# A four-layer graph network on one core: first pair transposed by TensorE, wk on SyncE's queue, half-array steps counted by the scheduler, leads by stage at the end

## The chip, the cores and the metric

The kernel runs on one core of one Trainium2 chip. A core has five engines, each with its own instruction stream: TensorE (PE, matrix multiplication, with weight loads shown apart as PEld), VectorE (DVE), ScalarE (ACT), GpSimd (POOL) and SyncE (SP), which here only issues DMAs. Streams are in order: an instruction that waits holds everything behind it on its engine. The metric is the device time of one execution in microseconds, lower is better; the time before is the median of three runs.

## The reference

`x` has 128 batches of a 128 x 512 matrix in fp32, `adj` is one 128 x 128 matrix shared by all batches and layers. Four layers follow each other, each with a residual and a layer norm.

```python
def reference(x, adj, b0, Wq, bq, Wk, bk, Wv, bv, Wo, bo, W, a, beta, weight, bias):
    # layer 0: out = max_j relu(A[:, None, :] + (C - A)[:, :, None]), A = adj @ x, C = A + b0
    x = layernorm(x + L0(x, adj, adj, b0))
    # layer 1: attention, 8 heads of 64
    q, k, v = (x @ Wq + bq), (x @ Wk + bk), (x @ Wv + bv)          # per head
    s = q @ k.T / sqrt(64) + (1 - adj) * -1e9
    x = layernorm(x + (softmax(s) @ v) @ Wo + bo)
    # layer 2: graph attention
    h = x @ W
    e = leaky_relu((h @ a[:512])[:, None] + (h @ a[512:])[None, :], 0.2) * adj
    x = layernorm(x + elu(softmax(e) @ h + beta * h))
    # layer 3: graph convolution, norm_adj = D^-1/2 adj D^-1/2
    x = layernorm(x + norm_adj @ (x @ weight) + bias)
    return x
```

Since in layer 0 the second operand is `adj` as well, the maximum over j is a row maximum of `adj @ x` plus a bias, and that is how the kernel computes it.

## The kernel before

Batches are worked in pairs (64 pairs, named by their even batch). Each batch passes through some hundred named steps; a step is one Python function that issues the instructions of one stage for one batch or pair. The steps on TensorE are:

- `A` (L733): `adj @ x`, two matmuls of 128 x 512.
- `QP1` to `QP7`, the same with `K`, `V`, `Y`, `U`, `Z` (all L644, in `seven`): a 256 x 512 by 512 x 512 product for a pair, done with seven half-size products in place of eight. `Y` is the product with Wo, `U` that with layer 2's W, `Z` that with layer 3's weight. Each step is 8 matmuls of 128 x 128 x 128 (`Q`, `K`) or 4 of 128 x 128 x 256 (the others). The seven products need differences of the weights, made once (`QT`, `KT`, ... four subtractions, L601 to L604), and sums of the operand (`XS1` to `XS4`, `YS1` ..., L620, on GpSimd). Results go into three small groups of PSUM tiles (`px` 1, `py` 2, `pz` 1), which ScalarE and VectorE read and combine (`u`, `U2`, `U3`, `C11` to `C22`, L657 to L703).
- `SC` (L807): the scores of one batch, 16 matmuls that contract over 64 rows only, two heads at a time in the two row halves of the array.
- `O` (L882): probabilities by v, 16 matmuls that fill 64 columns only, two heads in the two column halves.
- `E`, `BT` (L929, L967): one transpose each; `GT` (L980) and `NX` (L1027): 8 matmuls each, layer 2's attention by x and layer 3's norm_adj by x.

Between them lie the layer norms (`ST0`/`Y1`/`U3`/`Z1` on VectorE, `Q0` to `Q3` and `AP0` to `AP3` on ScalarE, `P0` to `P3` on GpSimd), the softmaxes (`M`, `SM1`, `EXP`, `SMR`, `SMN`), layer 2's logits (`L`, `EZ`, `E1`, `EE`, `E2`, `BE`), its elu (`U1`, `UE`, `U2`, `UP`) and evacuations (`OE`, `GE`, `NE`).

**Transposes by way of DRAM.** The layer-0 output of a batch is transposed thus: `MX1` (L757) stores it to DRAM in `dx`, `MX2` (L763) loads it back with four DMAs in 32-row blocks into `xB`, and `TX` (L782) transposes the blocks on VectorE into `xT`, which Q, K and V read. The probabilities go the same way (`MS1`, `MS2`, `TS`). `RL` (L771) loads a pair's `dx` a second time, as the residual `x2`, to which `C1` (L775, GpSimd) adds a bias row that `ROW` (TensorE, L493) and `ROW1` make from bv, Wo and bo.

**The order of the work** is written by a planner that runs while the program is built, `list_order`. Each `Step` has an engine, a cost in us, steps that it comes after (some with a delay in planned time), and buffers that it takes from `POOLS`. The planner places one step at a time: the one that can start earliest by its costs; on TensorE ties go by `rank` (`LAG`, a due time in batches for each step name), on the others by readiness less `soon`. The order that results is the instruction order of each engine; the delays and costs exist in the planner alone, and on the chip an instruction starts when its operands and buffers are there.

All x loads and transposes, and the weights from Wv on (`FETCH`), are issued by SyncE; Wq is issued by ScalarE at the start (L424), and the four DMAs of Wk by ScalarE after `AP0` of batch 1.

Of the kernel before, what the change touches and what calls it, by code (L numbers as in the profile page):

```python
# [23 lines left out]
SIGNAL = 0.2  # L24


class Step:
# [8 lines left out]
    def __init__(self, engine, cost, *after, takes=(), soon=0.0, batches=None, port=False):  # L36
        self.port = port or engine == "POOL"
        self.engine, self.cost, self.after = engine, cost, after
        self.takes, self.soon = dict(takes), soon
        self.batches = batches or (lambda b: True)  # L40
# [17 lines left out]
def list_order(steps, rank, pools, n):  # L58
# [13 lines left out]
    free, ends, taken, order = {}, {}, {p: [] for p in pools}, []  # L72
    while todo:
        best = None
        for k in can:
# [8 lines left out]
            key = (t, rank(*k) if s.engine == "PE" else ready[k] - s.soon, k)  # L84
# [5 lines left out]
        ends[k] = free[s.engine] = t + s.cost  # L90
# [24 lines left out]
def second(b):  # L115
    return b == 1
# [3 lines left out]
    "px": 1, "py": 2, "pz": 1, "tr": 2, "sc": 1, "x": 3, "xB": 2, "xT": 2,  # L120
    "qT": 2, "kT": 1, "v": 2, "s": 1,
    "sB": 1, "sT": 1, "oT": 1, "x2": 2, "z": 1, "e": 2, "bT": 2, "gT": 1, "m": 1, "x3": 2,
# [17 lines left out]
    "LD": Step("SP", 0.4, "LD-1", "MX1-2", takes={"x": ("MX1",)}),  # L140
# [7 lines left out]
    "AP0": Step("ACT", 1.03, "P0+"),  # L148
    "MX1": Step("SP", 0.4, "AP0", "MX1-1", takes={"dx": ("MX2+", "RL")}),
    "MX2": Step("SP", 1.8, ("MX1", 2.1), takes={"xB": ("TX",)}),  # L150
    "RL": Step("SP", 0.4, ("MX1+", 2.1), takes={"x2": ("UP+",)}, batches=even),
    "C1": Step("POOL", 1.27, ("RL+", 3.0), "ROW1@"),
    "TX": Step("DVE", 0.65, ("MX2", 2.9), "TX-1"),
    "SC": Step("PE", 1.2, takes={"sc": ("M",)}),
# [8 lines left out]
    "O": Step("PE", 1.15, "TS", "VE", "O-1", takes={"tr": ("OE",), "oT": ("Y+",)}),  # L163
# [33 lines left out]
    "WV0 WV1 WV2 WV3 WO0 WO1 WO2 WO3 BV BO W20 W21 W22 W23 A0 A1 BETA W30 W31 W32 W33 B3"  # L197
).split()
for i, name in enumerate(FETCH):
    STEPS[name] = Step("SP", 0.4, (FETCH[i - 1], 1.4) if i else "MX2+", batches=first)  # L200
STEPS["TX"].takes = {"xT": ()}

for i in range(4):
    STEPS[f"WK{i}"] = Step("ACT", 0.1, "AP0" if i == 0 else f"WK{i-1}", batches=second)
# [11 lines left out]
def seven_steps(n, sums, needs, weights, pool, out, add=(), turned=False, copy=False, T="POOL"):  # L216
# [20 lines left out]
    step("P1", "PE", c, "S1", *needs, (n + "T@",), takes={  # L237
        "px": (n + "C11",), "u": (last,), **({"uL": (n + "C21",)} if turned else {}), **out
    })
    step("P6", "PE", c, "S2", "P1", takes={"py": (n + "C21",)})  # L240
# [29 lines left out]
for n, needs, letters in (  # L270
    ("X", ["TX+"], "QKV"), ("Y", ["OE+"], "Y"), ("U", ["GE+"], "U"), ("Z", ["NE+"], "Z")
):
    sum_steps(n, needs, readers_of(*letters))
done = {
    "Q": seven_steps("Q", "X", ["TX+", "BQ@"], [("ADJ1", 9.0)], "xT", {"qT": ("SC+",)},
                     turned=True, T="DVE"),
    "K": seven_steps("K", "X", ["TX+", "BQ@"], [("WK3@", 4.0)], "xT", {"kT": ("SC+",)}, turned=True),
    "V": seven_steps("V", "X", ["TX+"], [("WV3", 4.0)], "xT", {"v": ("O+",)}, copy=True),
# [12 lines left out]
    "A": 0.484, "VP4": 4.350, "KP6": 4.536, "QP3": 6.105, "KP2": 6.393, "QP6": 6.543,  # L291
    "QP7": 6.580, "QP2": 6.783, "QP1": 6.839, "KP1": 7.155, "QP4": 7.239, "KP3": 7.490,
    "QP5": 7.598, "KP4": 7.761, "VP1": 7.807, "KP5": 7.914, "KP7": 8.090, "VP6": 8.158,
    "VP7": 8.220, "VP2": 8.342, "SC": 8.342, "VP5": 8.615, "VP3": 9.057, "O": 10.588,
    "YP5": 11.378, "YP7": 12.212, "YP1": 12.323, "YP6": 12.631, "YP2": 13.017,
    "YP4": 13.081, "YP3": 13.224, "E": 13.481, "UP5": 13.618, "BT": 13.636, "GT": 13.682,
    "UP6": 14.401, "UP2": 14.576, "UP4": 14.618, "UP3": 14.739, "UP1": 15.409,
    "UP7": 15.488, "NX": 16.433, "ZP4": 16.536, "ZP3": 16.847, "ZP6": 17.306, "ZP1": 17.589,
    "ZP2": 17.729, "ZP7": 18.238, "ZP5": 18.291,
}  # L300

LEAD = {}
# [9 lines left out]
def kernel(  # L312
# [464 lines left out]
    def TX(b):  # L777
        if b % 2 == 0:
            xT[b] = buf("xT", [P, C, 2 * P], b)
            xT[b + 1] = xT[b]  # L780
# [342 lines left out]
```

## Time and profile before

| what | value |
|---|---|
| median of three runs | 3124.65 us (3120.0, 3124.65, 3124.87) |
| the profiled execution, own time | 3119.54 us |
| its span in the trace | 3117.8 us |
| TensorE busy | 3062.5 us, 98% of the span |
| VectorE, ScalarE, GpSimd busy | 75%, 70%, 55% |
| mean granted TensorE clock | 0.996 |
| DMA | 313.45 MB, mean 101 GB/s |

The span runs from the first to the last instruction of the program, and the profiled execution's own time is 1.7 us more. Busy time of an engine counts its instructions alone. Matmuls overlap each other in the records (each is listed as longer than the distance to the next), so the distance from the start of one step to the start of the next is the better measure of what a step costs TensorE.

### The profile page before, as it was taken

How to read it: one execution, taken by the hardware profiler on the slowest of the kernel's cores; microseconds unless marked ns; L12 is line 12 of the kernel's file. 1: busy time of each engine (PE TensorE's matmuls, PEld its weight loads, DVE VectorE, ACT ScalarE, POOL GpSimd, SP SyncE). 2: the span in 40 equal slices, each digit the busy share in tenths (PEclk: the TensorE clock that was granted, in tenths of full speed). 3: DMA queues.
4: the chain of work that ended last, by engine and by line, in shares of the span. 5: the costliest groups of instructions: out<-in, count | busy, mean ns of one | idle time of the engine just before them, and what ended most of it. 6: DMA issues, size and time to landing. Idle time of an engine off the chain costs nothing.

```text
span 3117.8 us, 61619 instructions
## 1 busy us (share of the span) xinstructions
PE 3062.5 (98%) x21010; PEld 2704.0 (87%) x21010; DVE 2335.9 (75%) x5410; ACT 2196.1 (70%) x7234; POOL 1721.3 (55%) x1950
## 2 busy tenths in 40 slices
PE   7999999999999999999999999999999999999996
PEld 5888888888888888888888888888888888888975
DVE  5777777777777777777777777777777777777774
ACT  3677777776776777777777767767777777776664
POOL 4455555555555555555555555555556555555465
PEclk9999999999999999999999999999999999999998
DMA  7333332332323323333323223233233333232120
GB/s 209 124 109 100 105 100 91 109 102 95 107 94 106 102 95 104 100 100 104 102 90 111 99 96 107 94 105 102 96 104 100 102 103 102 91 111 85 62 73 29
DMA packets 236763, 313.45 MB, mean 101 GB/s; under 512 B 27936, under 2 KB 159136, under 8 KB 236448
## 3 DMA queue, kind: packets, MB, share of 16 engines
q1 hardware_dynamic: 234096, 307.40, 29.8%
q8 instruction: 166, 2.72, 0.4%
q10 hardware_dynamic: 2352, 2.10, 0.3%
q14 instruction: 149, 1.22, 0.1%
HBM read 175.18 MB, written 134.22 MB: 99 GB/s over the span
## 4 chain that ended last, share of the span: by engine, by line
PE 95%; DVE 2%; ACT 1%; POOL 1%; issue 1%; DMA 0%; SPq 0%; POOLq 0%; DVEq 0%; ACTq 0%
PE py_U L644 6%; PE py_Q L644 6%; PE py_K L644 5%; PE py_V L644 5%; PE py_Y L644 5%; PE py_Z L644 5%; PE ps_s L807 4%; PE ps_nx L1027 4%; PE ps_o L882 4%; PE px_Q L644 4%; PE px_U L644 4%; PE pz_Q L644 4%; PE pz_K L644 4%; PE pz_V L644 4%; PE ps_gT L980 4%; PE px_V L644 4%
## 5 line engine op out<-in xcount | busy, mean ns | idle before, releaser
L578 ACT ACTIVATE x<-x,off,rstd 128x512 f32<-128x512 f32 x512 | 416.6, 814 | 17.1
L838 ACT ACTIVATE s<-s,mx 128x128 f32<-128x128 f32 x1024 | 395.2, 388 | 7.2 <-issue 3.7
L550 DVE BATCH_NORM_STATS2 st<-x 128x6 f32<-128x512 f32 x512 | 346.5, 677 | 12.8 <-DMA x<-in_x 7.7
L573 POOL TENSOR_TENSOR rstd<-rstd,neg_half 128x2 f32<-128x2 f32 x256 | 178.8, 698 | 288.5 <-ACT rstd L559 288.0
L852 ACT ACTIVATE s<-s,sm 128x128 f32<-128x128 f32 x1024 | 313.0, 398 | 1.2 <-DVE sm L847 1.1
L1041 POOL TENSOR_TENSOR x<-x,b_bc 128x512 f32<-128x512 f32 x128 | 178.2, 1393 | 196.2 <-PE ps_nx L1027 196.2
L620 POOL TENSOR_TENSOR SX_V<-xT 128x256 f32<-128x256 f32 x128 | 93.3, 729 | 298.7 <-DVE sm L847 271.0
L916 DVE SCALAR_TENSOR_TENSOR junk<-x,wa_bc 128x512 bf16<-128x512 f32 x256 | 233.4, 912 | 32.3 <-ACT x L578 20.8
L1008 POOL TENSOR_TENSOR x<-x,x 128x512 f32<-128x512 f32 x128 | 162.9, 1272 | 76.2 <-DVE x L1004 67.8
L892 ACT COPY oT<-ps_o 128x512 f32<-128x512 f32 x128 | 75.0, 586 | 183.7 <-PE ps_o L882 182.1
L838 ACT ACTIVATION_READ_ACCUMULATOR s<-s,mx 128x1 f32 x1024 | 192.4, 188 | 0.0
L620 POOL TENSOR_TENSOR S_Y<-oT 128x256 f32<-128x256 f32 x128 | 93.8, 732 | 162.1 <-PE pz_U L644 157.4
L775 POOL TENSOR_TENSOR x<-x,bo_bc 128x512 f32<-128x512 f32 x128 | 160.4, 1275 | 24.5 <-DMA x<-dx 24.3
L577 ACT ACTIVATE off<-off,rstd 128x1 f32<-128x1 f32 x512 | 147.5, 288 | 27.4 <-POOL rstd L573 24.0
L823 DVE TENSOR_TENSOR s<-ps_s,mask 128x512 f32<-128x512 f32 x256 | 164.1, 681 | 1.8 <-PE ps_s L807 1.8
L703 DVE TENSOR_TENSOR x<-py_Y,x 128x256 f32<-128x256 f32 x192 | 81.5, 424 | 109.4 <-PE py_Y L644 82.9
L644 PEld LDWEIGHTS px_K<-xT,wk_sb 128*128 128x128 f32 x1024 | 133.7, 192 | 31.2 <-issue 27.0
L872 DVE STREAM_TRANSPOSE sT<-sB 128x1024 f32<-128x1024 f32 x128 | 158.1, 1235 | 0.8 <-PE ps_o L882 0.7
L1027 PE MATMUL ps_nx<-naT,x 128*128 128x128 f32 x1024 | 145.8, 288 | 13.0 <-ACT x L578 12.6
L807 PEld LDWEIGHTS ps_s<-kT,qT 64*128 64x128 f32 x2048 | 124.2, 187 | 38.4 <-issue 37.3
L832 DVE TENSOR_REDUCE mx<-s 128x8 f32<-128x1024 f32 x128 | 155.4, 1214 | 2.0
L1027 PEld LDWEIGHTS ps_nx<-naT,x 128*128 128x128 f32 x1024 | 133.7, 198 | 24.2 <-ACT x L578 13.6
(182 smaller groups left out, 9226.4 us busy)
## 6 DMA issues: line engine op xcount, KB each, us to landing
dp<-s SPq DMA_DIRECT2D x128, 512.0 KB, 2.6
sB<-dp SPq DMA_DIRECT2D x512, 128.0 KB, 2.8
x<-in_x SPq DMA_DIRECT2D x128, 256.0 KB, 3.3
dx<-x SPq DMA_DIRECT2D x128, 256.0 KB, 2.7
xB<-dx SPq DMA_DIRECT2D x512, 64.0 KB, 2.0
x<-dx SPq DMA_DIRECT2D x64, 512.0 KB, 3.2
out_x<-x SPq DMA_DIRECT2D x128, 256.0 KB, 2.0
wq_sb<-in_L_gnn_Wq ACTq DMA_DIRECT2D x4, 256.0 KB, 6.3
```

The costliest lines, as they stand in the source:

```text
L550: nc.vector.bn_stats(st, t)
L573: nc.gpsimd.tensor_tensor(r, r, neg_half.to_broadcast([P, 2]), ALU.pow)
L578: nc.scalar.activation(dst, src, AF.Identity, bias=shift, scale=scale)
L620: nc.gpsimd.tensor_tensor(s[:, i], x, y, op)
L644: nc.tensor.matmul(to, lhsT=one, rhs=two, start=(new and k == 0), stop=(k == 1), skip_group_check=True,)
L807: nc.tensor.matmul(scores[b][par][:, c, :], lhsT=qT[b][rows, c, cols], rhs=kT[b][rows, c, cols], start=True, stop=True,)
L823: nc.vector.tensor_tensor(by_head(s)[:, par * C : (par + 1) * C], ps.rearrange("p h (q s) -> p h q s", s=S), mask.rearrange("p (q s) -> p ...
L838: nc.scalar.activation(s[:, :, h], s[:, :, h], AF.Exp, bias=mx[:, h : h + 1], accum_out=sums[b][:, h : h + 1],)
L852: nc.scalar.activation(s[:, :, h], s[:, :, h], AF.Identity, scale=sm[:, h : h + 1])
L916: nc.vector.scalar_tensor_tensor(junk, x2[b][:, b % 2], 1.0, wa_bc[i], op0=ALU.mult, op1=ALU.mult, accum_out=s12[b][:, i : i + 1],)
L1027: nc.tensor.matmul(ps[:, c, :], lhsT=x3[b][:, b % 2, c * P : (c + 1) * P], rhs=naT, start=True, stop=True,)
L1041: nc.gpsimd.tensor_tensor(t, t, b3_bc, ALU.add)
```

## The change

There are four parts, and a new plan that comes from them.

1. **The first pair (batches 0 and 1) no longer goes through DRAM to be transposed.** `PX` (VectorE) copies x into the column order that `xT` has, `PT` (TensorE) makes four 128 x 128 transposes into one PSUM tile, and `PTE` (VectorE) copies that to `xT`. `MX2` and `TX` are left to batches from 2 on. `MX1` stays for all batches, since `RL` reads `dx`.
2. **The four DMAs of Wk move** from ScalarE's queue (after `AP0` of batch 1) to the head of `FETCH` on SyncE's queue; the planner starts `FETCH` after the first two x loads plus 4 us, each piece 1.3 us after the one before, and no longer after `MX2` of the first pair. `KT`, the weight differences of K, moves from GpSimd to VectorE.
3. **The planner knows half-array steps.** `SC` has the mode "row", `O` the mode "col", all others "". A step whose mode differs from the one before it on TensorE costs `SWITCH` = 0.1 us more in the plan (the costs of `SC` and `O` themselves are lowered from 1.2 and 1.15 to 1.09 and 1.02), and while a mode is on, another step with a mode is ranked `CLOSE` = 0.5 batches earlier.
4. **New due times.** `LAG` is replaced, and `LEAD`, empty before, holds values for single stages of pairs 56 to 63.

Beside these: four x buffers for three, three `x2` for two; `LD` waits in the plan for `LD` of two batches before plus 8 us in place of `MX1`; `MX2` is priced at 2.6 for 1.8; the need of the weight differences goes from `P1` to `P6`.

In the new order of instructions on TensorE, an `O` stands directly before an `SC` 104 times and an `SC` directly before an `O` 3 times; in the old one the latter happens twice and the former never. All other steps are the same in number, with 2 x 4 transposes added.

```diff
-    def __init__(self, engine, cost, *after, takes=(), soon=0.0, batches=None, port=False):
+    def __init__(self, engine, cost, *after, takes=(), soon=0.0, batches=None, port=False, mode=""):
...
-            key = (t, rank(*k) if s.engine == "PE" else ready[k] - s.soon, k)
+            if s.engine == "PE":
+                key = (t, rank(*k) - (CLOSE if mode and s.mode else 0.0), k)
+            else:
+                key = (t, ready[k] - s.soon, k)
...
-        ends[k] = free[s.engine] = t + s.cost
+        ends[k] = t + s.cost
+        if s.engine == "PE" and s.mode != mode:
+            ends[k] += SWITCH
+            mode = s.mode
+        free[s.engine] = ends[k]
...
-    "px": 1, "py": 2, "pz": 1, "tr": 2, "sc": 1, "x": 3, "xB": 2, "xT": 2,
+    "px": 1, "py": 2, "pz": 1, "tr": 2, "sc": 1, "x": 4, "xB": 2, "xT": 2,
...
-    "LD": Step("SP", 0.4, "LD-1", "MX1-2", takes={"x": ("MX1",)}),
+    "LD": Step("SP", 0.4, "LD-1", ("LD-2", 8.0), takes={"x": ("MX1", "PX")}),
...
-    "MX2": Step("SP", 1.8, ("MX1", 2.1), takes={"xB": ("TX",)}),
+
+    "PX": Step("DVE", 0.6, "AP0", takes={"xB": ("PT",)}, soon=20, batches=early, port=True),
+    "PT": Step("PE", 0.5, "PX", takes={"tr": ("PTE",)}, batches=early),
+    "PTE": Step("DVE", 0.65, "PT", "PTE-1", soon=20, batches=early),
+    "MX2": Step("SP", 2.6, ("MX1", 2.1), takes={"xB": ("TX",)}, batches=late),
...
-    "TX": Step("DVE", 0.65, ("MX2", 2.9), "TX-1"),
-    "SC": Step("PE", 1.2, takes={"sc": ("M",)}),
+    "TX": Step("DVE", 0.65, ("MX2", 2.9), "TX-1", batches=late),
+    "SC": Step("PE", 1.09, mode="row", takes={"sc": ("M",)}),
...
-    "O": Step("PE", 1.15, "TS", "VE", "O-1", takes={"tr": ("OE",), "oT": ("Y+",)}),
+    "O": Step("PE", 1.02, "TS", "VE", "O-1", takes={"tr": ("OE",), "oT": ("Y+",)}, mode="col"),
...
-    "WV0 WV1 WV2 WV3 WO0 WO1 WO2 WO3 BV BO W20 W21 W22 W23 A0 A1 BETA W30 W31 W32 W33 B3"
+    "WK0 WK1 WK2 WK3 WV0 WV1 WV2 WV3 WO0 WO1 WO2 WO3 BV BO W20 W21 W22 W23 A0 A1 BETA W30 W31 W32 W33 B3"
...
-    STEPS[name] = Step("SP", 0.4, (FETCH[i - 1], 1.4) if i else "MX2+", batches=first)
+    STEPS[name] = Step("SP", 0.4, (FETCH[i - 1], 1.3) if i else ("LD@", 4.0), batches=first)
...
-for i in range(4):
-    STEPS[f"WK{i}"] = Step("ACT", 0.1, "AP0" if i == 0 else f"WK{i-1}", batches=second)
...
-    "A": 0.484, "VP4": 4.350, "KP6": 4.536, "QP3": 6.105, "KP2": 6.393, "QP6": 6.543,
...
+    "A": 0.506, "QP4": 9.260, "KP1": 9.601, "QP1": 10.141, "QP6": 10.308, "QP2": 10.612,
...
-LEAD = {}
+LEAD = {
+    "Q56": 0.53, "U56": 0.07, "A57": -0.03, "BT57": -0.1, "GT57": -0.06, "NX57": 2.33,
...
-    return b + LAG[name] - LEAD.get(b // 2, 0.0)
+    stage = name[0] if name[1:2] == "P" else name
+    return b + LAG[name] - LEAD.get(f"{stage}{b // 2}", 0.0)
...
-    step("P1", "PE", c, "S1", *needs, (n + "T@",), takes={
+    step("P1", "PE", c, "S1", *needs, takes={
...
-    step("P6", "PE", c, "S2", "P1", takes={"py": (n + "C21",)})
+    step("P6", "PE", c, "S2", "P1", (n + "T@",), takes={"py": (n + "C21",)})
...
-            op = (nc.vector if n == "Q" else nc.gpsimd).tensor_tensor
+            op = (nc.vector if n in "QK" else nc.gpsimd).tensor_tensor
...
-        nc.sync.dma_start(out=dx[b][:, b % 2], in_=xs.pop(b))
+        nc.sync.dma_start(out=dx[b][:, b % 2], in_=xs[b])
...
+    def PX(b):
+        xB[b] = buf("xB", [P, Q, P], b)
+        nc.vector.tensor_copy(
+            xB[b].rearrange("p c (q s) -> p c q s", s=S),
+            xs[b].rearrange("p (q c s) -> p c q s", q=Q, s=S),
+        )
+
+    def PT(b):
+        ps = pa[b] = tr_tile(f"ps_x_{b}")
+        src = xB.pop(b)
+        for c in range(C):
+            nc.tensor.transpose(ps[:, c, :], src[:, c], ident)
+
+    def PTE(b):
+        if b % 2 == 0:
+            xT[b] = xT[b + 1] = buf("xT", [P, C, 2 * P], b)
+        nc.vector.tensor_copy(xT[b][:, :, (b % 2) * P : (b % 2 + 1) * P], pa.pop(b))
...
-    for i in range(4):
-        do[f"WK{i}"] = lambda b, i=i: fetch(nc.scalar, wk_parts[i])
```

## The prediction

> **What bounds the kernel now.** I read the page's busy shares first, then busy time by stretches, then TensorE's timeline where `SC` and `O` stand, then the waits of TensorE.
>
> ```profile
> span 3117.8 us, 61619 instructions
> PE 3062.5 (98%) x21010; PEld 2704.0 (87%) x21010; DVE 2335.9 (75%) x5410; ACT 2196.1 (70%) x7234; POOL 1721.3 (55%) x1950
> PE   7999999999999999999999999999999999999996
> ```
>
> TensorE is busy in every slice but the first and the last. By stretches (time, then busy us of each engine, granted clock, DMA share):
>
> ```profile
> 0.00:25.00 25.00, 10.04 (x16) 3.62 (x17) 12.17 (x31) 6.11 (x16) 2.05 (x11) 1.00 0.73 188
> 25.00:40.00 15.00, 8.27 (x47) 7.49 (x47) 3.37 (x8) 3.76 (x10) 12.37 (x13) 1.00 0.70 187
> 140.00:2985.00 2845.00, 2844.86 (x19700) 2525.86 (x19699) 2170.43 (x5023) 2054.82 (x6800) 1581.19 (x1787) 1.00 0.30 99
> 2985.00:3033.00 48.00, 43.11 (x263) 36.11 (x262) 34.42 (x81) 31.49 (x89) 32.60 (x38) 0.96 0.20 69
> 3033.00:3118.00 85.00, 57.80 (x265) 46.31 (x264) 40.95 (x100) 36.65 (x91) 47.62 (x54) 0.89 0.09 32
> ```
>
> For 2845 us TensorE never stops, so there only less TensorE work can help. Elsewhere it starves: the first 40 us and the last 130. In the timeline of TensorE (start, length in the records, step):
>
> ```profile
> 87.21 1.05 PE L644 MATMUL py_Q<-SX_V,QT 128*128 128x128 f32 x8
> 88.19 1.09 PE L882 MATMUL ps_o<-sT,v 128*64 128x128 f32 x16
> 89.22 1.16 PE L644 MATMUL px_Q<-xT,wq_sb 128*128 128x128 f32 x8
> 90.21 1.03 PE L644 MATMUL pz_V<-wv_sb,SX_V 128*128 128x256 f32 x4
> 91.08 1.05 PE L644 MATMUL py_Q<-xT,QT 128*128 128x128 f32 x8
> 92.06 1.16 PE L807 MATMUL ps_s<-kT,qT 64*128 64x128 f32 x16
> 93.15 1.09 PE L882 MATMUL ps_o<-sT,v 128*64 128x128 f32 x16
> 94.18 1.16 PE L644 MATMUL px_K<-xT,wk_sb 128*128 128x128 f32 x8
> 95.17 1.06 PE L644 MATMUL py_K<-SX_V,KT 128*128 128x128 f32 x8
> ```
>
> From start to start a Q or K step takes 0.89 us (68.10 to 68.99). Here the one ahead of the lone `O` takes 0.98 and the one after it 0.99, with `O` itself 1.03: a switch costs 0.09 before and 0.10 behind, beyond what is inside `O` and `SC`. Where `SC` and `O` are neighbours they take 1.09 and 1.03 as when alone, but there is one 0.09 and one 0.10 for both. One neighbourhood saves 0.197 us (0.094 + 0.103, the medians over the steady stretch).
>
> ```profile
> PE ps_nx L1027 <- ACT x L578: 12.6, 4, 5.2
> PE py_Q L644 <- POOL SX_V L620: 6.7, 1, 6.7
> ```
>
> These are the largest waits in the tail and in the head. Priced at steady distances (Q and K step 0.8915, other products 0.8645, `A` 0.86, `GT` and `NX` 0.891, transposes 0.109, `SC` 1.092, `O` 1.024, 254 entries and exits at 0.197, 4.5 for single steps), all of TensorE's work is 110.1 + 798.8 + 1549.2 + 228.1 + 27.9 + 139.8 + 131.1 + 50.0 + 4.5 = 3039.5 us. The span has 78.3 more: 30.1 lost by `A` of batch 4 at 39.1, 3.9 up to 2985, 35.5 up to the last product at 3108.1, 8.9 behind it.
>
> **What the Trainium skill says.** "TensorEngine Tiling (Array Packing)", section Key Properties, says that changing the tiling mode drains TensorE. The trace agrees: at 93.15 the first weight load of `O` starts 0.20 us after the last pair of `SC` matmuls, where pairs follow each other at 0.11. It doesn't say that a change between two tiled modes costs one drain; `SC` to `O` shows that, `O` to `SC` no trace shows. "TensorE: Matmul & The Clock Gate", Part 1, says that the clock halves after an idle window of about 3.4 us and recovers after as much work: `NX` of pair 124 comes after 5.2 us of waiting and the 16 matmuls of the two `NX` take 3.78 us, where two `NX` cost 2 x 0.891 at steady distances. "DMA: Bandwidth & Descriptors", section Issuing engines are not separate DMA queues, says that moving an issue between engines saves only issue time; so Wk gains by being earlier, not by its queue.
>
> **The change, part by part.**
>
> *Neighbours.* 107 in the new order against 2: 105 x 0.197 = 20.7 us less. From below: if `O` to `SC` drains twice, only the one more of the shown kind counts, 0.2 us. From above: drains fully shared, 0.1 to 0.2 more each, which the shown kind excludes. I take 20.7. The added transposes cost 8 x 0.11 = 0.9.
>
> *Head.* Before: x of batch 1 is normalized at 13.69 (L578), `MX1`, `MX2`, `TX` give `xT` at 25.86; but Wk, issued by ScalarE from 12.88, lands at 24.95, and GpSimd spends 25.07 to 30.37 on `KT` with the sums `XS1`, `XS2` behind it, so `QP6` starts at 32.56. After: `PX` is like the nearest row (tensor operation of 128x512 on VectorE, 0.69), so PX of batch 1 ends at 14.4; TensorE has `PT` of batch 0 to about 14.5, `A` of batch 2 (2.05 cold) to 16.5, `PT` of batch 1 to 17.5; `PTE` (0.69) ends at 18.3. Then VectorE, in order, does `R` (0.88) and `QT` and `KT` (4 x 0.69 each) to 24.8; the sums are ready by 21.3. If `PX` costs nothing or double, nothing moves: `PT` waits for `A`. `KP1` runs at 21.2, `KP2` at 24.5 after two ScalarE reads, then `A`, `VP1` (Wv is issued by about 19, lands after 6.7, as before), and `KP6` at 28.9 with 8.05 of work done: 20.9 lost by then, where before it was 30.1 by its counterpart. Gain so far 9.2. But moved issues come back. Three of Wk's DMAs stand in SyncE's queue ahead of x of batch 2 or 3, the fourth ahead of `MX1` of batch 1, at 0.45 us of issue each; and Wk's 1 MB now shares the DMA engines with Wq (1 MB) and four x (1 MB): 3 MB at the first slice's 209 GB/s are 14.4 us, and none of it is wanted before `R` ends at 19.2 but the first two x, which are issued first. If those came later, all of the head would by as much. `RL` now stands before three Wv pieces and x of batches 4 and 5, waits for `MX1` to land (2.7), and holds them. `AP0` of pair 2 waits for `P0`, which on GpSimd stands behind `VT` (5.1, from Wv at 25.7): `MX1` of batch 2 goes at about 33; x of batch 6 needs its buffer and waits for that to land; x of batch 8 goes at about 49, behind `MX2` of three batches (4 x 0.66 each), and lands 3.3 later, 2 us too late for its `A`. `XS2` of pair 2 stands behind `C1` of batches 2, 4 and 5, so behind two `RL`s: another 2. Hand-offs made adjacent (`QP2` to `VP1`, `VP6` to `VP7`) cost 1.4 and 0.7, the first `BT` chain about 1.5. Lost by 140: about 30, against 32.7. I take a gain of 2.5; from +8 (none of it comes back) to -6 (weights and x later still; the DMA share is 0.7 here).
>
> *Tail.* `NX` waits for the chain elu, residual, statistics, normalization after `UP3`. In pair 120 it took 16.8 us and had 12.4 of TensorE work beside it; the second `NX` 18.6 with 13.3. The new order puts 19.3 and 21.4 there: 5 us less. In pair 122 it took 17.6 with 13.8 beside it; the new order has 16.1: 2.2 less. In pair 124 16.8 with 8.3; the new order has 6.4: 1.9 more. From the last `Y` product on, both orders have 47.6 of work for a chain that took 84.3, so nothing changes. `E` to `BT` in pair 124 goes from 5.4 to 3.7 beside a chain of 8.2, up to 1.7 more; smaller waits of `ZP7` and `YP1` go, 2. Sum 5.6 gained; from 0 to 10.
>
> *Steady stretch.* All stages keep their work, so a pair takes 47.42 - 0.39 = 47.03 us if no hand-off leaks. In the old order five hand-offs from TensorE through one read back to TensorE leave under 0.25 us; `QP6` to `QP7` takes 1.64 (start of the one to the end of the read, 1.59, plus 0.05) with 1.78 of work there, and it never waited. In the new order about nine are so close: `UP6` to `UP7` takes 1.59 with 1.76 there (`UP6` and one K step), `QP2` to `YP1` takes 1.77 with 1.76 there (0.02 each pair), `GT` to the second `A` 1.73 with 1.89. I take 2 us in all; from 0 to 26. The deeper x and `x2` buffers cost no time; Wk's and `MX2`'s other prices only place steps.
>
> Sum against the profiled span: -20.7 + 0.9 - 2.5 - 5.6 + 2 = -25.9, so 3092 in the span and 3094 as its own time. The median shown is 5.1 over the profiled execution; 3124.65 - 26 is 3099. I take the middle, 3096.
>
> **Rivals.**
> 1. *Leaks eat part.* A tight hand-off needs its reader free: one read of 0.42 that comes 0.1 late in each of 60 pairs is 6 us. Three such: 3108 to 3116. For: twice as many tight places; against: none leaked before. 0.13.
> 2. *`O` to `SC` saves nothing.* Then 104 x 0.197 = 20.5 comes back: 3116. For: no record of it; against: its mirror image. 0.07.
> 3. *Slower.* VectorE stands behind one long instruction ahead of `UU2`, the read between `UP6` and `UP7`: there `TX` (0.70) stands in front of it, and `TX` waits for a DMA. If that comes late by over 0.43 us in each pair, 60 x 0.43 = 26 is lost and the kernel is level; at 1 us it is 3130. Against: the order has `MX2` a full pair earlier. 0.06.
> 4. *The moved loads hurt, or the stages' leads do nothing*: 3100 to 3105 by losing head and tail gains. 0.10.
>
> **How the numbers follow.** My forecast, 3086 to 3102, has 0.64. A measurement of this kernel tells 0.2%, 6.2 us, from no change: level is 3118.4 to 3130.9. Faster takes the forecast, cases 1, 2 and 4 but for 0.04 of them: 0.90. Level 0.04, slower 0.06. The range runs from 3083 (head and tail at their better ends, or runs like the profiled one) to 3117, which takes in cases 1, 2 and 4.
>
> **What would show it.** `SC` and `O` neighbours with 0.98 ahead of `O` and 0.99 behind `SC` only, and 47.0 us from pair to pair; else rival 2. Waits of TensorE between 140 and 2900 under 0.05 per pair; else rival 1 or 3, with the reader named. `KP6` near 29 us. `NX` of pair 120 without a wait, those of 124 and 126 still half-clocked. I am wrong if the steady pair takes over 47.2, or if the sum is right while head and tail differ by more than 6 us.

## The result: no change, and where the gain went

The changed kernel takes 3121.99 us in the median of 12 runs (3115.71 to 3123.77), the kernel before in the same sessions 3122.35 us (12 runs). The ratio is 0.9995, with a 95% interval from 0.9986 to 1.0004. The forecast was 3096, its range ended at 3117: it was wrong. The page of the changed kernel begins almost like the one before:

```profile
span 3119.8 us, 61689 instructions
PE 3059.5 (98%) x21018; PEld 2694.8 (86%) x21018; DVE 2303.2 (74%) x5416; ACT 2205.9 (71%) x7234; POOL 1676.2 (54%) x1946
PE   7999999999999999999999999999999999999996
```

In 40 slices of 78 us nothing is to be seen. The same stretches as in the prediction (time, busy us and instructions of TensorE, weight loads, VectorE, ScalarE, GpSimd, then granted clock, DMA share, GB/s) show it:

```profile
0.00:25.00 25.00, 12.78 (x34) 6.83 (x34) 15.67 (x35) 6.51 (x17) 6.24 (x15) 0.79 0.90 215
25.00:40.00 15.00, 14.28 (x79) 11.78 (x80) 6.84 (x17) 6.99 (x21) 7.63 (x7) 0.78 0.45 138
40.00:140.00 100.00, 87.83 (x603) 71.11 (x602) 71.77 (x156) 53.68 (x197) 41.64 (x42) 0.97 0.57 174
140.00:2985.00 2845.00, 2837.20 (x19754) 2515.79 (x19753) 2130.59 (x5025) 2068.64 (x6819) 1540.97 (x1794) 1.00 0.30 99
2985.00:3033.00 48.00, 46.82 (x281) 39.66 (x281) 35.09 (x79) 30.39 (x87) 33.03 (x37) 1.00 0.20 63
3033.00:3120.00 87.00, 60.57 (x273) 49.65 (x272) 43.30 (x106) 39.66 (x97) 46.71 (x53) 0.87 0.07 25
```

TensorE now works from 13 us on, with short stops, and through the second row, where before it had 8.27 of 15 us. But from 40 to 140 us it is busy for 87.83 us, where the kernel before had 98.39:

```profile
40.00:140.00 100.00, 98.39 (x728) 84.63 (x727) 74.60 (x168) 63.32 (x232) 45.51 (x49) 1.00 0.55 170
```

In the stretch in which it never stopped it now stands 7.8 us. The tail's first stretch is better, 46.82 for 43.11. The clock column of the first two rows (0.79 and 0.78, 1.00 before the change) is not read as a cause: in the kernel before, with 1.00 there, the record of `A` of batch 2 at 17.61 is 2.07 us long, where 1.02 is usual, so the column doesn't show all slow steps.

To put a number on each stretch I count as "lost" what the prediction counted: the start of a step on TensorE, less the work ahead of it at steady distances. All of this work is 3039.4 us before and 3019.6 after (104 + 3 neighbours, eight transposes more).

| stretch | lost before | lost after | change | forecast |
|---|---|---|---|---|
| up to 45 us | 30.1 | 23.4 | -6.7 | |
| 45 to 563 us | 3.2 | 28.7 | +25.5 | |
| start and first pairs together | 33.3 | 52.1 | +18.8 | -2.5 |
| 563 to 2985 us | 0.7 | 8.9 | +8.2 | +2 |
| 2985 us to the end | 44.4 | 39.2 | -5.2 | -5.6 |
| TensorE's work itself | 3039.4 | 3019.6 | -19.8 | -19.8 |
| sum (the span) | 3117.8 | 3119.8 | +2.0 | -25.9 |

The neighbours, the very start and the tail came as forecast. 25 us were lost again between 45 and 563 us, and 8 in the steady stretch. Of TensorE's waits over the whole run these are the largest (us in total, times, longest), two for inputs at the very start left out:

```profile
PE ps_nx L1075 <- ACT x L609: 10.5, 2, 5.7
PE ps_a L764 <- DMA x<-in_x: 6.6, 3, 4.1
PE py_Q L675 <- DVE qT L727: 5.5, 3, 3.0
...
PE pz_K L675 <- DVE kT L727: 2.8, 1, 2.8
```

The two waits for VectorE are new. From 40 to 560 us, VectorE waits for this (`st` are the row sums of step `ST0`), first after and then before the change:

```profile
DVE st L581 <- DMA x<-in_x: 18.9, 14, 3.5
```

```profile
DVE st L550 <- DMA x<-in_x: 1.7, 3, 0.9
```

and in the waits of SyncE's queue in the same stretch the load of x (L411, L380 before) waits for the store `MX1` to land (`dx<-x`):

```profile
SPq L411 <- DMA dx<-x: 41.1, 26, 4.9
```

```profile
SPq L380 <- DMA dx<-x: 8.4, 11, 1.5
```

A load of x takes the buffer that an `MX1` gives back. In the new order `LD(b)` stands on SyncE close behind `MX1(b-4)`, the very store that reads its buffer (from batch 12 on directly or with one step between, for batches 8 to 11 with three to eight), and the queue stands until that store has landed. In the old order two to fifteen steps lie between `MX1(b-3)`, whose buffer it was, and `LD(b)`. The planner frees a buffer when `MX1` is issued, not when it lands. So x comes late, and since the plan knows nothing of it, VectorE has the sums of the late batch in front of reads that TensorE needs. A case in full, in the timeline of VectorE (start, length, step, in brackets the idle time and its releaser):

```profile
266.00 0.69 DVE L581 BATCH_NORM_STATS2 st<-x 128x6 f32<-128x512 f32 x1 [0.50 <-DMA x<-in_x]
...
269.21 0.69 DVE L581 BATCH_NORM_STATS2 st<-x 128x6 f32<-128x512 f32 x1 [1.87 <-DMA x<-in_x]
269.94 0.18 DVE L582 BATCH_NORM_AGGREGATE mv<-st 128x2 f32<-128x6 f32 x1
270.04 0.39 DVE L727 SCALAR_TENSOR_TENSOR kT<-pz_K,kT 128x256 f32<-128x256 f32 x1
```

and in TensorE's:

```profile
270.48 1.97 PE L675 MATMUL pz_K<-SX_V,wk_sb 128*128 128x128 f32 x8 [2.77 <-DVE kT L727]
272.25 1.91 PE L675 MATMUL px_V<-wv_sb,xT 128*128 128x256 f32 x4
```

The read of `pz_K` could not run while the sums waited for x; `KP3` of pair 12 waited 2.77 us for it, and this step and the next ones run at half clock after it (1.77 us to the next start, where 0.89 is usual). The whole stall is 4.6 us (2.9 + 0.9 + 0.8). That is the theory to be tested, "late x at the head of VectorE's line". The rivals: TensorE wants the late x itself; the loads are slow, not late; the stalls come with the start and not with the order.

### The profile page after: what moved, and what is told of

It is laid out like the page before. It is cut to its first block, busy times and chain, and to the rows that moved or that the text cites. A ratio compares the mean times of both kernels' runs of the same rounds, so it can differ in the third digit from the quotient of the medians.

```text
span 3119.8 us, 61689 instructions
## 1 busy us (share of the span) xinstructions
PE 3059.5 (98%) x21018; PEld 2694.8 (86%) x21018; DVE 2303.2 (74%) x5416; ACT 2205.9 (71%) x7234; POOL 1676.2 (54%) x1946
## 4 chain that ended last, share of the span: by engine, by line
PE 91%; DMA 3%; DVE 2%; ACT 2%; issue 1%; POOL 0%; SPq 0%; POOLq 0%; DVEq 0%; ACTq 0%
PE py_Y L675 5%; PE py_U L675 5%; PE py_V L675 5%; PE py_Q L675 5%; PE py_Z L675 5%; PE py_K L675 5%; PE ps_s L855 4%; PE ps_o L930 4%; PE px_U L675 4%; PE ps_nx L1075 4%; PE pz_Q L675 4%; PE px_V L675 4%; PE px_Y L675 4%; PE ps_gT L1028 4%; PE pz_Y L675 3%; PE pz_Z L675 3%
## 5 line engine op out<-in xcount | busy, mean ns | idle before, releaser
L1089 POOL TENSOR_TENSOR x<-x,b_bc 128x512 f32<-128x512 f32 x128 | 163.2, 1276 | 255.4 <-PE ps_nx L1075 254.2
L651 POOL TENSOR_TENSOR S_U<-gT 128x256 f32<-128x256 f32 x128 | 107.1, 836 | 228.0 <-ACT gT L940 228.0
L964 DVE SCALAR_TENSOR_TENSOR junk<-x,wa_bc 128x512 bf16<-128x512 f32 x256 | 184.2, 719 | 16.1 <-ACT x L609 10.6
L734 DVE TENSOR_TENSOR x<-py_U,u_U 128x256 f32<-128x256 f32 x192 | 81.1, 422 | 103.8 <-PE py_U L675 53.7
L675 PEld LDWEIGHTS px_Q<-xT,wq_sb 128*128 128x128 f32 x1024 | 129.3, 192 | 26.4 <-issue 23.7
L675 PEld LDWEIGHTS py_K<-SX_V,KT 128*128 128x128 f32 x1024 | 129.8, 193 | 24.5 <-issue 23.4
L855 PE MATMUL ps_s<-kT,qT 64*128 64x128 f32 x2048 | 148.9, 285 | 0.0
L1075 PE MATMUL ps_nx<-naT,x 128*128 128x128 f32 x1024 | 138.4, 280 | 10.5 <-ACT x L609 10.5
```

Source lines behind the costliest of these rows:

```text
L651: nc.gpsimd.tensor_tensor(s[:, i], x, y, op)
L675: nc.tensor.matmul(to, lhsT=one, rhs=two, start=(new and k == 0), stop=(k == 1), skip_group_check=True,)
L855: nc.tensor.matmul(scores[b][par][:, c, :], lhsT=qT[b][rows, c, cols], rhs=kT[b][rows, c, cols], start=True, stop=True,)
L964: nc.vector.scalar_tensor_tensor(junk, x2[b][:, b % 2], 1.0, wa_bc[i], op0=ALU.mult, op1=ALU.mult, accum_out=s12[b][:, i : i + 1],)
L1075: nc.tensor.matmul(ps[:, c, :], lhsT=x3[b][:, b % 2, c * P : (c + 1) * P], rhs=naT, start=True, stop=True,)
```

## The experiments

Most are the changed kernel with single steps moved in its list (`move(step, after=...)` takes a step out of the planner's list and puts it behind another), since a planner run with one constant changed writes another order altogether. Ten of them do the same work as the changed kernel up to 40 us; the start of `KP6` lies between 29.3 and 31.7 us in these. So differences of less than about 2 us in the first pairs are not read. All but the last four runs are one execution each, and the twelve of the changed kernel lie 8 us apart. So what is read is the loss in a stretch, and not the span alone. Where an experiment left the later steps as they are, 7.9 to 9.7 us are lost from 563 to 2985 us, and 35.9 to 40.3 us behind that.

**The steady stretch: one step, one place later.**

```diff
+for b in range(10, 106, 2):
+    move(("YP1", b), after=("ZP5", b - 6))
```

> The changed kernel with one edit: from pair 10 to pair 104 TensorE's step YP1 stands one place later, behind ZP5 of the pair three before, so that QC11's copy has one more TensorE step (about 0.5 us) to end before YP1 wants it. If the steady stretch leaks because YP1 waits for QC11 (0.015 us late in each pair, and YP1 itself then 0.103 us longer), the period of a pair falls from 47.17 to about 47.05 us, YP1 shows no wait, and the span is 5 to 6 us shorter than the changed kernel's 3119.8. If the 0.10 us belongs to YP1's place among the steps and not to its wait, the period falls by no more than 0.02 us and the span by under 1 us.

The span is 3112.9 us. From `KP1` of pair 20 to that of pair 104, a pair takes 47.063 us, where it took 47.194 (47.43 before the change); 3.3 us are lost from 563 to 2985 us instead of 8.9. The first expectation holds. In the timeline of TensorE in the changed kernel, `YP1` is `px_Y`:

```profile
1381.24 1.03 PE L675 MATMUL py_Z<-ZT,nx 128*128 128x256 f32 x4
1382.12 1.13 PE L675 MATMUL px_Y<-wo_sb,oT 128*128 128x256 f32 x4
1383.09 1.03 PE L675 MATMUL pz_Z<-w_sb,S_Z 128*128 128x256 f32 x4
```

and with the step moved:

```profile
1378.79 1.03 PE L675 MATMUL pz_Z<-w_sb,S_Z 128*128 128x256 f32 x4
1379.65 1.03 PE L675 MATMUL px_Y<-wo_sb,oT 128*128 128x256 f32 x4
1380.51 0.27 PE L1015 MATMUL ps_bT<-ident,e 128*128 128x128 f32 x1
```

`px_Y` costs 0.97 us in the first and 0.86 in the second. The timeline of the weight loads in the changed kernel says why:

```profile
1382.12 0.73 PEld L675 LDWEIGHTS px_Y<-wo_sb,oT 128*128 128x128 f32 x4 [0.25 <-ACT qT L688]
```

and with the step moved:

```profile
1379.43 0.84 PEld L675 LDWEIGHTS px_Y<-wo_sb,oT 128*128 128x128 f32 x4
```

The first weights of `px_Y` are loaded at 1382.12, together with its first matmul; with the step moved they are loaded 0.22 us ahead of it. It is the wait and not the place: in the changed kernel itself `YP1` of pair 108 stands behind the same step `ZP4`, comes on time and costs 0.863 us (at 2655.35). The Trainium skill, "TensorE: Matmul & The Clock Gate", Part 2, says that weight loads are pulled ahead of running matmuls. It doesn't say what a wait on another engine does to this: here it stops the weights too. A hand-off that is 0.015 us late costs 0.12.

**The neighbours taken apart.**

```diff
+for b in range(12, 118):
+    # where O stands directly ahead of SC, SC goes behind the next step
+    move(("SC", b), after=pe[i + 1])
```

> The changed kernel with the neighbours taken apart: wherever O stands directly ahead of SC on TensorE (batches 12 to 117), SC goes one step later, so that a full-array step lies between them again; nothing else moves. If each pair of neighbours saves one change of mode of 0.197 us, about 0.39 us comes back in each pair: a period of some 47.55 us in place of 47.17, and a span 18 to 21 us longer, near 3139. If neighbours save nothing (a change between the two half-array modes costs as much as one to the full array), the period and the span stay within 1 us.

The span is 3139.6 us, 19.8 more than the changed kernel's, and a pair takes 47.574 us, 0.38 more. The loss up to 563 us (51.1) and up to 2985 us (59.7) stays. In the changed kernel:

```profile
1368.35 1.03 PE L675 MATMUL pz_U<-w_sb,S_U 128*128 128x256 f32 x4
1369.30 1.09 PE L930 MATMUL ps_o<-sT,v 128*64 128x128 f32 x16
1370.33 1.16 PE L855 MATMUL ps_s<-kT,qT 64*128 64x128 f32 x16
1371.42 1.13 PE L675 MATMUL px_U<-w_sb,gT 128*128 128x256 f32 x4
1372.39 1.03 PE L675 MATMUL pz_U<-w_sb,S_U 128*128 128x256 f32 x4
```

and taken apart:

```profile
1376.27 1.03 PE L675 MATMUL pz_U<-w_sb,S_U 128*128 128x256 f32 x4
1377.23 1.09 PE L930 MATMUL ps_o<-sT,v 128*64 128x128 f32 x16
1378.25 1.13 PE L675 MATMUL px_U<-w_sb,gT 128*128 128x256 f32 x4
1379.32 1.16 PE L855 MATMUL ps_s<-kT,qT 64*128 64x128 f32 x16
```

A step of 0.86 us costs 0.95 ahead of `O` and 0.97 behind `SC` in the first; in the second `px_U` between the two costs 1.07 us (1378.25 to 1379.32), since it bears the exit of one mode and the entry of the other. In all 101 places were taken apart, at 0.196 us each. The gain of the neighbours is there in full.

**The first pairs: the sums later.**

```diff
+for b in range(27, 11, -1):          # ST0 one to four places later on VectorE
+    move(("ST0", b), after=dve[i + n])
+for b in (8, 9):
+    move(("A", b), after=("QP1", 2)); move(("R", b), after=("TX", 4))
+    move(("ST0", b), after=("VC12", 0))
```

> The changed kernel with VectorE's row sums ST0 of batches 8 to 27 one to four places later in VectorE's order (and TensorE's A and R of batches 8 and 9 later to match), so that the reads of other steps that stand behind ST0 no longer wait while ST0 waits for its load of x; the loads themselves are where they were. If the stalls of the first pairs come from ST0 at the head of VectorE's line, most of those at A of batch 8 (4.4 us with 1.8 at half clock), VP5 and YP5 of pair 2, QP7 of pair 8, QP4 of pair 10 and KP3 of pair 12 go, and the loss at 563 us falls from 52 to about 40, the span to 3106 to 3110. If these stalls are TensorE's own want of x (its steps read the late x themselves), they move with the steps and the loss stays above 48.

The span is 3107.0 us, 12.8 less, and the loss at 563 us is 41.9. VectorE's waiting for x from 40 to 560 us went from 18.9 us to this:

```profile
DVE st L581 <- DMA x<-in_x: 6.5, 5, 2.1
```

The loads themselves stand where they stood (SyncE's order was not touched). Of the 10.2 us less at 563 us, 4.2 come before 80 us, where TensorE's `A` of batches 8 and 9 was moved too; in the changed kernel `A` of batch 8 waited 4.11 us for its own x. There the edit can't tell the theory from the first rival. The other 6.0 come from 80 to 563 us, where the sums alone were moved: 9.1 us are lost in place of 15.1, and 8.3 in a second kernel with the same edits up to there (the second of the mends together, below). `KP3` of pair 12 loses 0.7 us in place of 4.6. So 6 to 7 us of the loss were VectorE's line, with the late load only as its start; for these the theory holds and the first rival falls. The last 2.6 us of the shorter span come behind 563 us, where nothing was moved, and are not read.

**The first pairs: slots for x that nobody still reads.** The tile `nx` (4 KB for each partition) is used from 210 us on; the x of four batches goes into it, so each of the loads of batches 8 to 19 takes a slot of two batches earlier.

```diff
 def LD(b):
-    xs[b] = buf("x", [P, D], b)
+    if b in (8, 14):
+        t = buf("nx", [P, 2, D], f"x{b}")
+        xs[b], xs[b + 1] = t[:, 0], t[:, 1]
+    elif b not in (9, 15):
+        xs[b] = buf("x", [P, D], b)
```

> The changed kernel, instructions in the same order, with the x of batches 8, 9, 14 and 15 in the tile nx that nothing else uses until 210 us, so that the loads of batches 8 to 19 take a slot whose last reader was done one pair earlier, in place of one that the store directly ahead on SyncE still reads. If the loads are late because SyncE waits for that store to land (2 to 5 us each), the loads of these batches land that much sooner, VectorE's wait for x falls from 18.9 us between 40 and 560 us to under 8, and the loss at 254 us falls from 46 to 38 to 42; the stall at KP3 of pair 12, whose x comes later, may stay. If the loads are slow for the share of the DMA engines, or late for their place behind other waits on SyncE, the loss at 254 us stays above 44.

The wait of SyncE for the stores is halved, VectorE's wait for x is 13.6 us in place of 18.9:

```profile
DVE st L585 <- DMA x<-in_x: 10.0, 8, 2.0
...
DVE st L585 <- DMA nx_x<-in_x: 3.6, 2, 2.3
```

```profile
SPq L415 <- DMA dx<-x: 21.6, 18, 2.8
```

The loss at 254 us is 41.6 (45.0 to 47.1 in the changed kernel and two others with its order up to there), the span 3116.0. The loss answers as expected; VectorE's wait fell less than that. From 60 us on the loads are not slow in themselves: those issued up to 563 us land after 2.9 us (median) in the changed kernel, and after 3.4 in the kernel before. Before 60 us they are slower: 5.0 us (2.6 to 8.7) after and 4.0 (2.8 to 5.2) before, so for `A` of batch 8 the second rival isn't excluded. The skill, "DMA: Bandwidth & Descriptors", section Anatomy of one DMA (of a DMA issued by GpSimd), says that DMA engines don't wait on semaphores: the wait lies with the issuing engine. That agrees with these 41.1 and 21.6 us on SyncE, behind which all of its later transfers stand.

What remains is place or landing, so the loads of batches 8 to 17 were also moved ahead on SyncE:

```diff
+for b, after in ((8, ("MX1", 5)), (9, ("LD", 8)), (10, ("LD", 9)), (11, ("MX1", 6)), (12, ("MX2", 6)), ...):
+    move(("LD", b), after=after)
```

> The kernel with the x of batches 8, 9, 14 and 15 in the tile nx, and besides it the loads of x of batches 8 to 17 earlier in SyncE's order: x of batch 8, 9 and 10 right behind MX1 of batch 5, the others one to three places ahead of where they stood. If what is left of the late loads (13.6 us of VectorE's and 8.4 us of TensorE's waiting for x between 40 and 560 us) comes from their place behind other waits on SyncE, the stall at A of batch 8 (3.2 us and 2.1 at half clock behind it) goes, VectorE's wait falls to 5 to 9 us, and the loss at 254 us is 35 to 38 in place of 41.6. If the DMA engines are what is slow there (x of batch 8 landed 7.0 us after its issue), A of batch 8 still waits over 2 us and the loss at 254 us stays above 40.

The wait of `A` of batch 8 is gone: its x is issued at 46.2 us and lands after 4.3 us, where in the changed kernel it was issued at 51.95 and took 7.0 (this one load was both late and slow). But the loss at 254 us is 43.4 and the span 3116.4: nothing was gained, against what I expected. In the timeline of VectorE:

```profile
51.49 0.41 DVE L738 TENSOR_TENSOR v<-py_V,u_V 128x256 f32<-128x256 f32 x1
55.09 0.71 DVE L834 STREAM_TRANSPOSE xT<-xB 128x512 f32<-128x512 f32 x1 [3.18 <-DMA xB<-dx]
55.72 0.38 DVE L731 SCALAR_TENSOR_TENSOR qT<-py_Q,uL_Q 128x256 f32<-128x256 f32 x1
```

Now `TX` waits 3.18 us for the load of `xB`, and the reads of Q stand behind it; the second half of `SC` of batch 0 waits 2.92 us. `QP7` of pair 2, which waits behind `LOG` (next experiment), also lost 1.8 us more than with the slots alone. In the first pairs SyncE's queue has weights, stores, x and `xB` to issue in order; what goes forward pushes something back.

**LOG in two halves.** `LOG` is one piece of 8.6 us on VectorE at 67 us, and `QP7` of pair 2 waits 2.98 us behind it.

```diff
-    def LOG():
-        for i in range(2):
+    def LOG(i):   # LOG(0) where LOG stood; LOG(1) behind QC22 of pair 2, LOG1b, LOG2b, UT behind it
```

> The changed kernel with VectorE's LOG (67.0 to 75.6 us, 8.6 us in one piece with POOL's work beside it) cut into its two halves, the second behind the copy that QP7 of pair 2 waits for, and what reads the second half moved behind it. If LOG at the head of VectorE's line is what holds QP7 (3.2 us of waiting and 1.7 at half clock behind it), that stall shrinks to under 1 us, and the loss at 80 us falls from 37 to about 32; the span is 4 to 5 us shorter if later stalls don't take it back. If QP7 waits for its operand for another reason, its stall stays over 2.5 us.

At 80 us 33.3 are lost in place of 37.0: the stall of `QP7` went. But at 100 us it is 42.1 in place of 37.0, and the span is 3121.2. TensorE's timeline shows where it came back:

```profile
82.23 1.16 PE L676 MATMUL py_K<-SX_V,KT 128*128 128x128 f32 x8 [2.65 <-DVE qT L728]
87.47 0.65 PE L557 MATMUL ps_wa<-ident,wa_col 128*128 128x128 f32 x4 [2.36 <-DVE r L771]
94.66 1.12 PE L765 MATMUL ps_a<-x,adjT 128*128 128x512 f32 x2 [1.37 <-DVE r L771]
```

The second half stood ahead of other reads. The cause of the stall is shown, the mend failed.

**RL out of the way.**

```diff
+move(("RL", 0), after=("BO", 0))
```

> The changed kernel with pair 0's RL moved on SyncE behind BO, past the loads of Wv and of x4 and x5; in the changed kernel RL waits there for the landing of MX1 until 19.2 us and these loads stand behind it. If that hold sets the start, Wv's pieces leave 5 us earlier, KP6 starts near 25 us in place of 29.5, and about 4 us less is lost by then; the end is 4 us earlier if nothing later takes it back, and unchanged if the late loads of x that come after 50 us set the pace of the first pairs anyway (then the loss at 127 us stays near 40). If the start is set by the turning of the first pair and VectorE's sums instead, KP6 stays within 1 us of 29.5.

`KP6` starts at 26.53 us, 2.9 earlier than in the changed kernel, and 19.4 us are lost at 45 us in place of 23.4. By 127 us it is 38.9 (38.7 in the changed kernel), by 563 us 55.2, and the span is 3120.7. At 80 us it is still 3.3 us ahead. What takes it back is `YP5` of pair 0 at 124.94, which waits 2.83 us for VectorE (1.52 in the changed kernel) and runs at half clock; just before, VectorE's sums had waited 2.70 and 0.97 us for x. A start that is 3 us better is worth nothing while later loads set the pace.

**The tail: no leads.** `LEAD` empty, all else as changed.

> The changed kernel with the table of leads of the last pairs empty; steps up to the first of them are in the same order. If the leads are what shortened the end (44.4 us lost from 2985 us on before the change, 39.1 after), the loss there goes back by 4 to 7 us and the span is near 3125. If the tail gained from elsewhere (the neighbours alone), the span stays within 1 us of 3119.8.

The span is 3133.3 us, 13.5 more. From 2985 us on 49.6 us are lost, where the changed kernel loses 39.2 and the kernel before 44.4; the other 3 us are lost earlier, most of them in the first pairs, where both orders are the same. `NX` of the last pairs, in the changed kernel:

```profile
3074.40 3.78 PE L1075 MATMUL ps_nx<-naT,x 128*128 128x128 f32 x16 [4.78 <-ACT x L609]
3098.13 3.78 PE L1075 MATMUL ps_nx<-naT,x 128*128 128x128 f32 x16 [5.67 <-ACT x L609]
```

and without leads:

```profile
3085.05 3.79 PE L1063 MATMUL ps_nx<-naT,x 128*128 128x128 f32 x16 [4.78 <-ACT x L597]
3109.96 3.78 PE L1063 MATMUL ps_nx<-naT,x 128*128 128x128 f32 x16 [6.96 <-ACT x L597]
```

The leads are worth about 10 us, with the scatter of the tails 9 to 14. Without them the new order's tail is some 5 us worse than the old one. The forecast had the net of the two right.

**Single parts of the change, each with a plan of its own.** First the kernel before with the counting alone (modes, `SWITCH`, `CLOSE`, the costs of `SC` and `O`):

> The kernel before with the scheduler's new counting of changes of mode alone: the old start, the old queue for the weights, no leads. With the old due times it sets O directly ahead of SC in 28 places and not in 107. If each place is worth 0.197 us and the start is as before, the span is about 5 us shorter than the 3117.8 of the kernel before, near 3112, and the loss by 140 us stays near 33. If the stalls of the first pairs come with the new order of steps and not with the new start, the loss by 563 us is over 40 here too.

The span is 3131.3 us, 13.5 more than the kernel before. The 28 neighbours are there and TensorE's work is 5.1 us less, but 42.3 us are lost by 563 us (33.3 before), 2.3 more by 2985 and 52.4 behind it (44.4 before). By 127 us it was 34.7 (32.1 before): the old start is all but intact. So a new order opens stalls in the first pairs without the new start too. Then the new start alone, with the old costs and due times:

```diff
-SWITCH = 0.1
-CLOSE = 0.5
+SWITCH = 0.0
+CLOSE = 0.0
-    "SC": Step("PE", 1.09, mode="row", takes={"sc": ("M",)}),
+    "SC": Step("PE", 1.2, takes={"sc": ("M",)}),
...
 # and O's cost, LAG and LEAD as before the change
```

> The kernel before with the new start alone: the first pair turned by TensorE, the weights' queue, the four x buffers and three x2 of the changed kernel, but the old counting of TensorE's costs, the old due times and no leads. If the new start makes the stalls of the first pairs, the loss by 563 us is near the changed kernel's 52, after a start with KP6 near 29.5 us; with the steady stretch and the end of the kernel before, the span is then near 3130. If the new counting and due times make them, the loss by 563 us stays near 33 or falls below it by the 9 us that the start gains, and the span is 3107 to 3118.

The span is 3253.8 us: a miss for both. Up to 45 us 20.2 are lost, by 254 us 54.4, so the start makes stalls of its own; but the steady pair takes 49.49 us, and this order is no measure of the start alone. What it does show is the mechanism at full size. VectorE waits for x 61 times from 563 to 2985 us, and TensorE behind it:

```profile
DVE st L569 <- DMA x<-in_x: 91.0, 61, 3.7
```

```profile
1081.78 1.13 PE L663 MATMUL py_V<-VT,SX_V 128*128 128x256 f32 x4 [2.04 <-DVE v L722]
```

The hold on SyncE comes with the new start, to which the rule for `LD` belongs: from 40 to 560 us the loads wait 43.0 us for stores to land here, and 8.3 with the counting alone. How the 25.5 us divide between the new start and the new order stays open: the planner's answer to each part alone is another order.

**The mends together.** The first has the four edits above (`YP1`, `RL`, the sums, `LOG`):

> The changed kernel with the four edits together: YP1 one place later in the steady pairs, RL of pair 0 behind BO, the sums ST0 later, LOG in two halves. If the head's loss is the sum of these hold-ups, they add: about 5 (YP1), 10 to 12 (sums), 4 to 5 (LOG) and 0 to 4 us (RL), a span of 3095 to 3101 and a time of about 3098 to 3104, that is 0.6 to 0.8 per cent faster than before the change. If the loads of x set the pace of the first pairs, whatever stands where, only YP1's 5 us are left: a span near 3114 and a time near 3116.

It takes 3108.15 us, a ratio of 0.9957 to the kernel before (0.9941 to 0.9974), span 3105.8. Since `LOG` and `RL` had gained nothing alone, the second has only the other two:

> The changed kernel with the two edits that gained alone: the sums ST0 of batches 8 to 27 later in VectorE's order, and YP1 one place later in the steady pairs. If the losses are separate they add: the span is 12.8 + 6.9 us under 3119.8, near 3100, the time near 3102, and the ratio to the kernel before 0.9935. If one hides the other, or if cutting LOG and moving RL in the run with all four edits were not what cost the rest there, the span is 3105 to 3107.

3106.53 us, ratio 0.9953 (0.9936 to 0.9969), span 3105.7. `YP1` gives its 5 us (2.6 lost from 563 to 2900 us, 7.8 with the sums alone); but 44.5 are lost by 563 us where the sums alone had 41.9, and the tail loses about 1 more. That 2.6 came at `QP7` of pair 2, behind `LOG`, which lost 3.9 us here and 1.2 there. The edits up to there are the same, so it is the scatter of the first 80 us; from 80 to 563 us the two lose 8.3 and 9.1. With the slots as well:

> The changed kernel with the sums ST0 later, YP1 one place later and the x of batches 8, 9, 14 and 15 in the tile nx. If late loads still cost something once the sums stand later (6.5 us of VectorE's waiting are left), this is 1 to 4 us under the kernel with the two order edits alone, a span near 3097; if not, the two are equal within 1 us.

3107.21 us, 0.9954 (0.9939 to 0.9969), span 3105.1: equal. And with the loads moved ahead:

> The same with the sums ST0 of batches 12 to 27 later on VectorE and YP1 one place later in the steady pairs. If the loads ahead of time and the sums are two ways to take away the same wait, this is 1 to 3 us under the 3105.1 us of span of the run with the slots, the sums and YP1 (3102 to 3104), most of it at A of batch 10. If the loads in front push something else back on SyncE, it is 3105 or more.

3108.69 us, 0.9956 (0.9940 to 0.9973), span 3106.6: nothing more. The mends of x don't add to the later sums (from 80 to 563 us 8.8 and 8.5 us are lost with them, 8.3 without), which fits two ways around the same wait. All four beat the kernel before by 0.43 to 0.47%, and two order edits are enough for it. The spans of 3105 to 3107 us give back about half of the 28 us by which the forecast was missed.

## Why the prediction was wrong, by its own steps

- *Neighbours, -20.7 and +0.9*: right. `O` to `SC` shares its drain like `SC` to `O`. Taking them apart costs 19.8 us; rival 2 falls.
- *Head, start*: right. `KP6` at 29.47 us with 21.4 lost; I had 28.9 and 20.9. `VP1` and `VP7` waited 1.6 and 0.75 for 1.4 and 0.7.
- *Head, what comes back*: this step failed. "Lost by 140: about 30" was 40.5, and I took the first pairs as over there, while 11.6 more went by 563 us. I had counted the moved loads one by one, each with its own lateness (x of batch 8 "2 us too late": its `A` lost 4.4, and 1.8 more at half clock). What I left out is who stands behind a waiting instruction. On SyncE: I did follow `RL`, `MX2` and the `LD` of batch 6 there, but not that the loads of x wait for the landing of the stores close before them all through the first pairs (41.1 us from 40 to 560 us, 8.4 before the change); "the deeper x and `x2` buffers cost no time" passed over the one thing that the new `LD` rule does to the order. On VectorE: `ST0` with the late x ahead of the reads, 6 to 7 us by the experiments. And `LOG`, which stood at 67 us with `QP7` behind it, wasn't looked at: 3.2 us and 1.7 at half clock. Together these are some 18 of the 25.5 us; the rest lies in smaller waits that no run took apart.
- *Tail, -5.6*: right in its sum (-5.2), and `NX` of pairs 120 and 122 wait no more, as forecast. Its parts are larger than I saw: the leads give 10, the new order without them takes 5. Beside this, the `NX` with 5.2 us of waiting that the prediction calls pair 124's is that of pair 126 (at 3096.07); that of pair 124 waited 4.17.
- *Steady stretch, +2*: the place was right, "`QP2` to `YP1`, 0.02 each pair", and the size wrong. The term is 0.015 us of wait and 0.10 of restart in each pair; the experiment gave back 5.6 of the 8.9 us.
- *Rivals*: the fourth, "the moved loads hurt", named the cause, but I let it take back only the gains that I had counted, 3100 to 3105, as if a start could not become worse than before. The third, a long instruction on VectorE that waits for a DMA ahead of a read, is the mechanism that did it, with `ST0` in place of `TX` and in the first pairs in place of the steady ones. What was priced for each pair at 0.43 us was 2 us for each pair in the start-alone kernel. (The rival's 3130 for 1 us is a slip: by its own sum 60 us come on top of 3096.)

## What to carry to other kernels

Where an engine's order is fixed ahead, ask of every instruction that waits for a DMA what stands behind it in that order: here a late load cost its own step (`A` of batch 8) and, at the head of VectorE's line, the reads of other steps as well. A planner that frees a buffer when the store is issued puts the next load right behind that store, and the queue then waits for the landing. One more slot, or the landing time in the plan, would be the remedy at that place; no run tried the second, and the slots tried here halved the queue's wait and brought nothing on top of the later sums. A gain at the start is only kept if the resource that sets the pace behind it (here SyncE's queue and VectorE's line) isn't loaded by the same edit.

## What I had not expected of the hardware

- A TensorE step that waits 0.015 us for another engine loses 0.10 us besides, since its first weight load isn't pulled ahead; that is as much as leaving a half-array mode costs (0.10).
- The clock halves after shorter waits than I reckoned with, and their length alone does not decide. The skill, "TensorE: Matmul & The Clock Gate", Part 1, says about 3.4 us of idle; here steps ran at half clock after waits of 2.10 (`RL` moved, at 155.51), 2.56 (with the sums later), 2.77 and 2.98 us, but not after 2.65 (`LOG` in halves), 2.92 (loads ahead) or 3.58 us (the slots with the sums and `YP1`, at 73.23). What does decide stays open. At `QP7` of pair 2 the half clock alone is 1.7 us, a part of the scatter of the first pairs.
- `LOG`'s products (128x512, two inputs) take 0.69 us alone or where they start ahead of GpSimd (at 73.23), and 1.10 or 1.63 where GpSimd was at work before them (those that start at 70.81 and 73.96 take 1.63; GpSimd's `UT` instructions run from 70.19 to 71.90, 73.34 to 75.04 and from 75.12 on). The skill, "SBUF — State Buffer", section SBUF: two separate sides, says that VectorE with two inputs and a GpSimd instruction that reads SBUF exclude each other on one port for a whole instruction. The numbers are in line with that; no run here took GpSimd's work away to show it.
